# Attention of a graph layer taken two steps at a time, with three of four copies on ScalarE

## The chip, the cores and the metric

The kernel runs on one core of a Trainium2 chip. The core has five engines with a queue each: TensorE (PE; its weight loads are shown as PEld), VectorE (DVE), ScalarE (ACT), GpSimd (POOL), and SyncE (SP), which only issues transfers here. PE writes its results into PSUM, which has eight banks; DVE and ACT carry them from there to SBUF. The metric is the device time of one execution in microseconds (us), as the median over several runs. Times of single instructions come from one profiled execution.

## What is computed

There are 384 nodes with 1024 features. Two graph layers follow each other, each on a normalised and rectified input and with a residual. The first is an attention with 16 heads of 64 features and a mask made from the edges; the second is a relational convolution, two sublayers deep. Cut to what matters here:

```
h  = relu(layernorm(x))
q2 = (h wq' + bq) wiq' + biq ;  k2, v2 in the same way       (384 x 1024 each)
mask[src, dst] = softplus(w)[edge_type - 1], else -inf       (384 x 384)
attn = softmax(q2 k2' / 8 + mask)                            (per head, 384 x 384)
x  = x + (attn v2) wo' + bo
x  = x + relational_convolution(relu(layernorm(x)))          (counts A per relation and edge)
```

All numbers are fp32.

## The kernel before

Nodes are split into three blocks of 128. Queues are written out by hand for PE, POOL, SP and DVE, and from the attention on for ACT too: each engine works through its instructions in the order of the program text. So the order of calls in the text is the order in each queue.

The projections make q2, k2 and v2. The function `second_v` multiplies one half (512 columns) of one node block of v2, and gives back the copy out of PSUM.

The attention is then a run of 24 steps. Step g stands for pair p = g // 3 of heads (two heads, 0 and 1, in the two halves of the 128 partitions) and block m = g % 3. For each step there are these pieces of work:

- `scores(g)`: PE multiplies q2's block by k2 for both heads. The two products go to banks 0 and 1 for an even g, to banks 2 and 3 for an odd one. The two heads run in the array side by side.
- `exponents(g)`: DVE adds the mask to the scores and finds the extreme of each row in one operation per head (s, L576); ACT takes the exponential of each head (L579), and sums the rows. The result lies in one of eight slots for probabilities, in the tiles prA and prB.
- `normalise(g)`: DVE takes the reciprocal of the two sums (L584), and scales each head (L586).
- `turn_probs(g)`: PE transposes, for each head, block m of the three steps of pair p (three transposes each), into one of the banks 4, 5 and 6 in turn (L597). A copy brings the tile into a quarter of At (L598): on DVE for head 0, on ACT for head 1. Six transposes and two copies a step.
- `gather(g)`: PE multiplies v2's block m by the turned probabilities of each head (L608), and sums the three blocks of a pair in bank 7. After the third, ACT empties the bank into attT (L611), and the next pair starts in the same bank.

The loop runs over g with a lead of 5: it turns step g, does the exponentials of step g+5, normalises step g+4, computes the scores of step g+6, and multiplies step g-1 by v2. Ahead of it, steps 0 to 5 get their scores, in twos, with one piece of v2 after each of the first two pairs. Just before the last product, seven of eight parts of two blocks of ps_y = attT wo' are done (`multiply_o`, L615), which need the earlier pairs only.

In step 17 of the loop transfers are issued. SP loads w_x (which takes the place of q2 and k2), then five tiles w_c for the convolution (which take the place of w_o), then two slices of A, the table of edge counts. POOL loads the other slices and adds the second table to all of them. A has six slices, one for a relation, and its tables are filled by POOL's scatters (L266), which run through the whole attention.

After the attention come the output product, the normalisation, and the convolution, whose first sublayer needs the products ps_g (L840, L846) from PE, and from DVE the mixes of A (L326), the differences of weights (L787, L789, L795), and the additions into H (L853, L861, L863). POOL normalises the slices of A (L342).

## Time and profile before

| | |
|---|---|
| median of three runs | 737.99 us (736.06 to 738.41) |
| profiled execution | 735.77 us |
| its span, first to last instruction | 734.0 us |
| PE busy | 713.5 us (97%) |
| DVE busy | 472.9 us (64%) |
| ACT busy | 147.2 us (20%) |
| POOL busy | 323.3 us (44%) |
| first scores to the end of the last product with v2 | 237.4 to 317.7 us |
| first transposes to the first ps_y | 255.96 to 310.70 us |
| loads of A issued on SP | 388.1 us |

Times in the trace count from the start of the span. The chain is the work that ended last, followed back from the last instruction by what released each step. An fp32 product shows as two matmul records. A wait is put down to the releaser that came last. Shares of busy time are means over stages that differ much, so a change in one stage is read from that stage.

### The profile page before, as it was taken

What the parts mean: (1) busy time and instruction counts of PE and PEld (TensorE: products, weight loads), DVE (VectorE), ACT (ScalarE), POOL (GpSimd) and SP (SyncE); (2) the same over time, 40 slices, a digit from 0 to 9 for tenths busy, and PEclk for the clock granted to TensorE, in tenths of its full rate; (3) what the DMA queues carried; (4) which work ended last, traced back from release to release, by engine and by line L of the source; (5) the groups of instructions that cost most, each with busy time, mean ns of one, the idle gap of its engine ahead of it and who ended that gap; (6) DMA issues with size and microseconds to landing.
All of it is one profiled execution on the core that took longest, in us unless ns stands there. A gap on an engine that the chain in (4) does not pass through costs nothing.

```text
span 734.0 us, 8299 instructions
## 1 busy us (share of the span) xinstructions
PE 713.5 (97%) x3024; PEld 496.8 (68%) x3024; DVE 472.9 (64%) x1228; ACT 147.2 (20%) x338; POOL 323.3 (44%) x242
## 2 busy tenths in 40 slices
PE   8999989999999999999999999899999999999995
PEld 8759989999964444445995555555555555579943
DVE  6895897877504499625424779990187676506756
ACT  3201111111111477510131131100013111001100
POOL 1456777788886788587784454310000000030000
PEclk9999999999999999999999999999999999999999
DMA  7797766743447322623527953321003123700001
GB/s 296 261 346 231 221 182 209 212 148 115 116 119 240 59 1 2 215 0 47 127 2 169 312 163 129 129 83 46 0 1 107 66 85 129 271 29 1 1 29 57
DMA packets 40533, 90.96 MB, mean 124 GB/s; under 512 B 19644, under 2 KB 27680, under 8 KB 36270
## 3 DMA queue, kind: packets, MB, share of 16 engines
q1 hardware_dynamic: 18478, 79.62, 30.9%
q0 software_dynamic: 21008, 8.42, 10.4%
q10 hardware_dynamic: 1008, 2.41, 0.9%
q8 instruction: 23, 0.38, 0.2%
q14 instruction: 16, 0.13, 0.1%
HBM read 79.27 MB, written 11.16 MB: 123 GB/s over the span
## 4 chain that ended last, share of the span: by engine, by line
PE 86%; DVE 11%; ACT 1%; issue 1%; DMA 1%; DVEq 0%; ACTq 0%
PE ps_g L846 13%; PE ps_g L840 10%; PE ps_c L897 6%; PE ps_c L880 6%; PE ps_q L395 6%; PE ps_v L524 6%; PE ps_k L377 6%; PE ps_c L947 6%; PE ps_v L377 5%; PE ps_y L615 5%; PE ps_f L1054 4%; DVE same L250 3%; PE ps_q L377 3%; PE ps_x L377 3%; PE ps_o L608 2%; PE ps_s L563 2%
## 5 line engine op out<-in xcount | busy, mean ns | idle before, releaser
L266 POOL DMA_INDIRECT atab<-count,at x99 | 160.0, 1616 | 50.6 <-DMA atab<-count,at 26.2
L261 POOL DMA_INDIRECT mtab<-m_val,at x99 | 104.1, 1052 | 57.0 <-issue 24.4
L1041 POOL TENSOR_TENSOR x_sb<-x_sb,room 128x1024 f32<-128x1024 f32 x3 | 7.0, 2347 | 158.1 <-DMA room<-in_rows 158.1
L326 DVE SCALAR_TENSOR_TENSOR At<-A,small_sb,At 128x1152 f32<-128x1152 f32 x40 | 62.9, 1635 | 0.0
L840 PE MATMUL ps_g<-T,S 128*128 128x384 f32 x144 | 49.1, 486 | 0.0
L846 PE MATMUL ps_g<-w_c,XT 128*128 128x384 f32 x144 | 48.0, 487 | 0.0
L846 PE MATMUL ps_g<-w_c,XN 128*128 128x384 f32 x144 | 47.6, 486 | 0.0
L897 PE MATMUL ps_c<-At,H 128*128 128x384 f32 x144 | 46.6, 486 | 0.0
L395 PE MATMUL ps_q<-hT,w_q 128*128 128x384 f32 (+1 forms) x160 | 41.8, 422 | 1.4 <-ACT hT L90 1.4
L524 PE MATMUL ps_v<-w_v,v 128*128 128x512 f32 x96 | 41.9, 594 | 0.0
L840 PEld LDWEIGHTS ps_g<-T,S 128*128 128x128 f32 x144 | 27.4, 190 | 19.1
L897 PEld LDWEIGHTS ps_c<-At,H 128*128 128x128 f32 x144 | 27.4, 190 | 19.1
L846 PEld LDWEIGHTS ps_g<-w_c,XN 128*128 128x128 f32 x144 | 27.4, 190 | 19.1
L846 PEld LDWEIGHTS ps_g<-w_c,XT 128*128 128x128 f32 x144 | 27.2, 190 | 19.2 <-DVE H L861 0.6
L395 PEld LDWEIGHTS ps_q<-hT,w_q 128*128 128x128 f32 x160 | 28.5, 190 | 14.1 <-ACT hT L90 1.7
L377 PE MATMUL ps_k<-T,S 128*128 128x192 f32 x192 | 35.8, 330 | 0.0
L615 PE MATMUL ps_y<-w_o,attT 128*128 128x512 f32 x80 | 35.0, 595 | 0.0
L576 DVE CUSTOM_DVE_ANT_0 s<-ps_s,mask 128x384 f32<-128x384 f32 x48 | 24.5, 548 | 15.4 <-PE ps_s L563 15.4
L342 POOL TENSOR_TENSOR A<-A,rn 128x1152 f32<-128x1152 f32 x6 | 19.4, 3236 | 31.7 <-DVE rn L341 31.7
L524 PEld LDWEIGHTS ps_v<-w_v,v 128*128 128x128 f32 x96 | 18.0, 190 | 22.6 <-issue 22.6
L377 PEld LDWEIGHTS ps_k<-T,S 128*128 128x128 f32 x192 | 32.7, 194 | 0.0
L1054 PE MATMUL ps_f<-w_out,XN 128*128 128x512 f32 (+1 forms) x84 | 31.1, 531 | 0.0
(250 smaller groups left out, 1316.6 us busy)
## 6 DMA issues: line engine op xcount, KB each, us to landing
w_c<-in_basis SPq DMA_DIRECT2D x24, 768.0 KB, 6.2
atab<-zero SPq DMA_DIRECT2D x12, 576.0 KB, 8.2
A<-atab POOLq DMA_DIRECT2D x10, 576.0 KB, 9.8
w_c<-in_root SPq DMA_DIRECT2D x6, 768.0 KB, 5.5
w_q<-in_wq SPq DMA_DIRECT2D x4, 1024.0 KB, 11.8
w_q<-in_wiq SPq DMA_DIRECT2D x4, 1024.0 KB, 10.1
w_k<-in_wk SPq DMA_DIRECT2D x4, 1024.0 KB, 7.0
w_k<-in_wik SPq DMA_DIRECT2D x4, 1024.0 KB, 6.2
```

The source lines that it names most:

```text
L261: nc.gpsimd.indirect_dma_start(mtab[c // PER][:, :], bass.IndirectOffsetOnAxis(at[:, 0, c:c + 1], 0), m_val[:, c:c + 1], None)
L266: nc.gpsimd.indirect_dma_start(atab[0 if i < 18 - DEALT else i % 2][:, :], bass.IndirectOffsetOnAxis(at[:, 1, c:c + 1], 0), count[:, 1, c: ...
L326: nc.vector.scalar_tensor_tensor(At[:, b], A[:, r], w, At[:, b], ALU.mult, ALU.add)
L377: nc.tensor.matmul(ps, a[:, k, :], b[:, k, :], start=start and k == 0, stop=(k == 3), skip_group_check=not start)
L395: nc.tensor.matmul(ps[o][:, c], wt_[:, k, o * P:(o + 1) * P], src[:, k, c], start=(k == 0 and c.start == 0), stop=(k == KD - 1 and c.stop ...
L524: nc.tensor.matmul(ps, v[:, k, t * P:(t + 1) * P], w[k // 4][:, k % 4, :], start=(k == 0), stop=(k == KD - 1))
L615: nc.tensor.matmul(ps, attT[:, k, t * P:(t + 1) * P], w_o[half][k // 4][:, k % 4, :], start=(k == 0), stop=(k == KD - 1))
L840: nc.tensor.matmul(ps, x[:, c], y(c), start=start and c == 0, stop=(c == 2), skip_group_check=not start)
L846: nc.tensor.matmul(ps, block(XT, n, i)[:, c], w[c][:, i, o * HC:(o + 1) * HC], start=(first and c == 0), stop=(c == 2 and (i == 1 or ps is ...
L880: nc.tensor.matmul(pr[o], w[k // 2][:, k % 2, o * P:(o + 1) * P], XT[:, k, :], start=(k == 0), stop=(k == KC - 1 and l == L - 1))
L897: nc.tensor.matmul(pr[o], H_[:, b, n, o * P:(o + 1) * P], At[:, b, n, :], start=False, stop=(b == B - 1 and n == NT - 1))
L1054: nc.tensor.matmul(p, XT[:, k, t * P:(t + 1) * P], w[k // 2][:, k % 2, c0:c1], start=(k == 0), stop=(k == KC - 1))
```

## The change

The loop takes two steps at once. For an even g it turns steps g and g+1, does the exponentials of g+6 and g+7, normalises these two, computes the scores of g+8 and g+9, and multiplies steps g-2 and g-1 by v2. On DVE and ACT the copies of step g+1 stand between the exponentials of f = g+6 and those of f+1. Of the four copies of a double step DVE keeps one (step g+1, head 0). The slots for probabilities become twelve, the last four of them in slices 0 to 2 of A. All three blocks of v2's second half go between the first scores, and steps 0 to 7 get their scores ahead of the loop. The loads of A are issued after the loop; w_x and w_c stay in it, behind the last scores.

```diff
             for half in range(2):
                 w = [wload(wiv[half, j], "w_v2") for j in range(2)]
-                for t in range(NT - 2 * half):
+                for t in range(NT - NT * half):
                     second_v(half, t, w)()
...
         def probs(g):
-            i = g % 8
-            return (prA if i < 4 else prB)[:, 2 * (i % 4):2 * (i % 4) + 2, :]
+            i = g % 12
+            tile_ = (prA, prB, A.rearrange("p r t n -> p (r t) n"))[i // 4]
+            return tile_[:, 2 * (i % 4):2 * (i % 4) + 2, :]
...
-                (nc.scalar.copy if j else nc.vector.tensor_copy)(turned(g)[:, j, :], ps[:, :N])
+                copy = nc.vector.tensor_copy if g % 2 and j == 0 else nc.scalar.copy
+                yield lambda j=j, ps=ps, copy=copy: copy(turned(g)[:, j, :], ps[:, :N])
...
-        LEAD = 5
-        for f in (0, 2):
+        LEAD = 6
+        for f in (0, 2, 4):
             scores(f)
             scores(f + 1)
-            put_v = second_v(1, f // 2 + 1, w)
+            put_v = second_v(1, f // 2, w)
             for i in (f, f + 1):
                 exponents(i)
                 if i:
                     normalise(i - 1)
             put_v()
-        scores(4)
-        scores(5)
-        exponents(4)
-        normalise(3)
-        for g in range(STEPS + 1):
+        scores(6)
+        scores(7)
+        normalise(5)
+        for g in range(0, STEPS + 2, 2):
             f = g + LEAD
             if g < STEPS:
-                turn_probs(g)
+                copies = []
+                for i in (g, g + 1):
+                    for copy in turn_probs(i):
+                        copy() if i == g else copies.append(copy)
             if f < STEPS:
                 exponents(f)
-            if f - 1 in total:
-                normalise(f - 1)
-            if f + 1 < STEPS:
-                scores(f + 1)
+                copies.pop(0)()
+                copies.pop(0)()
+                exponents(f + 1)
+                normalise(f)
+                normalise(f + 1)
+            elif g < STEPS:
+                for copy in copies:
+                    copy()
+            if f + 2 < STEPS:
+                scores(f + 2)
+                scores(f + 3)
             if g == STEPS:
                 ps_y = [next_bank("ps_y", range(7)) for _ in range(2)]
                 multiply_o(ps_y[0], 0, 0, range(KD - 1))
             if g > 0:
+                gather(g - 2)
                 gather(g - 1)
-            if f + 2 == STEPS:
+            if f + 4 == STEPS:
...
-                for r in range(2):
-                    nc.sync.dma_start(A[:, r], tabs[0][r])
-                for r in range(R):
-                    nc.gpsimd.dma_start(A[:, r], tabs[1][r], accum_op=ALU.add)
...
+        for r in range(2):
+            nc.sync.dma_start(A[:, r], tabs[0][r])
+        for r in range(R):
+            nc.gpsimd.dma_start(A[:, r], tabs[1][r], accum_op=ALU.add)
```

## The prediction

> **What bounds the kernel now.** I read the page's busy times and chain first. TensorE (PE) is busy 97% and carries 86% of the chain, so the question is what PE waits for in the attention. Next the stretch that the diff touches, cut into stages (columns: stretch; time; PE, weight load, DVE, ACT, POOL busy; clock; DMA; GB/s):

> ```profile
> 237.36:255.96 18.60, 18.60 (x57) 7.98 (x57) 7.48 (x28) 8.15 (x20) 14.44 (x10) 1.00 0.40 58
> 255.96:270.60 14.64, 14.47 (x82) 7.06 (x80) 14.43 (x51) 10.80 (x32) 11.95 (x8) 1.00 0.20 1
> 270.60:299.97 29.37, 29.37 (x171) 13.64 (x169) 28.73 (x100) 23.31 (x67) 24.54 (x16) 1.00 0.23 2
> 299.97:304.30 4.33, 3.27 (x23) 1.67 (x21) 4.12 (x14) 3.18 (x9) 1.55 (x1) 1.00 0.94 321
> 304.30:310.70 6.40, 6.40 (x42) 3.34 (x40) 2.23 (x4) 2.50 (x5) 2.00 (x2) 1.00 1.02 396
> ```

> The third stage is the steady state, twelve steps of 2.447 us: PE is full, DVE 98%, ACT 79%. The chain in order of time (start, time, what) shows how a step is made, and one place where two steps' scores stand together:

> ```profile
> 237.43 1.49 PE ps_s L563 x8
> ...
> 282.11 0.80 PE ps_o L608 x4
> 282.91 0.81 PE ps_pT L597 x6
> 283.71 0.85 PE ps_s L563 x4
> ```

> A step's score group costs 0.85, two groups together 1.49: each change of kind costs PE about 0.1. In the single starts, scores follow each other 0.42 after a change and 0.316 within a run, transposes 0.165 and then 0.109, and the product with v2 0.367 after a change. From the last issue of a kind to the next kind it is 0.20 (transposes), 0.41 (scores), 0.42 (products).

> Last, rows of the timeline with the waits that PE already has (in brackets: idle time before, and its releaser), and the durations of the copies (least, median, most):

> ```profile
> 303.50 0.87 PE L608 MATMUL ps_o<-At,v 128*64 128x384 f32 x4 [1.06 <-ACT attT L611]
> ...
> L598 DVE COPY At<-ps_pT x24: 536/550/558, 257.2 to 309.7; 128x384 f32<-128x384 f32 x24
> L598 ACT COPY At<-ps_pT x24: 452/479/481, 257.3 to 310.1; 128x384 f32<-128x384 f32 x24
> ...
> 476.18 2.31 PE L880 MATMUL ps_c<-XT,w_c 128*128 128x384 f32 x6 [2.19 <-DVE H L853]
> ```

> The first row is the danger: the first product of a pair waits until ACT has emptied bank 7 of the pair before (L611). From start to next start in the trace: DVE's s (L576) 0.475, reciprocal 0.19, each L586 0.335, copy 0.467; ACT's exponential 0.61, copy and attT 0.463 (attT is done after 0.56). A waiting engine starts 0.05-0.06 after its releaser ends; ACT's exponential starts 0.66 after its s.

> [...] at 302.8 attT stands behind two exponentials although its product was long done. [...] 479 against 550 ns for a copy. [...] All pairs' products go through bank 7 alone, before and after. [...] 7 of the 48 L586 rows take 0.66-0.75 instead of 0.41.

> **The change, part by part.** *Work that only moves.* One second half of v2 (16 matmul records, 6.87) goes from before the scores into the score run, and steps 0-5 are now done under v2 instead of 0-4. The first scores start 6.87 earlier (230.5), the mask is ready at 232.6, so DVE loses 1 us under a v2 product of 7: nothing. The first transposes start after four score groups (1.49 each) and three v2 products (7.07 each): 230.49 + 27.15 = 257.64, against 255.96 before.

> *PE without waits.* A double step has 12 transposes (0.165 + 10x0.109 + 0.20 = 1.46), 4 score slots (0.42 + 2x0.316 + 0.41 = 1.47) and 4 product slots (0.367 + 2x0.316 + 0.42 = 1.42; the 0.316 is taken from the scores, at worst 0.367): 4.35 instead of 2x2.447 = 4.89. Over nine double steps with scores and three without this would save about 5.7.

> *The new loop DVE-PE.* DVE's order in a double step is s(f) twice, copy (step g+1, head 0), s(f+1) twice, normalise f and f+1. The copy needs the third transposed tile, and s(f+1) stands behind the copy. With the first transpose at 0: the tile's last transpose issues at 0.165 + 7x0.109 = 0.93 and ends at 1.20; copy 1.26; s(f+1) 1.73 and 2.20, the second has read its bank at 2.75. PE's scores f+3 overwrite that bank (a step's two heads use banks 0-1 or 2-3 by g's parity): head 1 starts at 2.80, second pass 3.22, products 3.63, next transposes 5.05. PE alone would be there at 4.35. So a double step takes 5.05 instead of 4.89. Behind the waiting copy stand s(f+1) and both normalisations, and for s(f+1) wait the scores, behind which stand the products. Before, the scores of a step overwrote the bank that DVE had read a step earlier, so the copy ahead of s did not matter to them.

> *The new load on ACT.* Copies 0.60 and 1.07, exponentials f 1.53 and 2.14 (they now stand behind copies that wait for this double step's transposes), copy 2.74, exponentials f+1 3.21 and 3.81, done 4.51. DVE then normalises f+1: reciprocal 4.56, free at 5.44; s(f+2) to 6.39, where the next copy was due at 6.31: 0.08 late. Hence about 5.1. The fourth transposed tile needs the first of three banks back (copy ends 1.08): 0.09, inside the loop's slack.

> *Bank 7.* Products come in twos (g-2, g-1), so in one double step of three a pair's last and the next pair's first stand side by side (2|3, 8|9, 14|15, 20|21). The last pass of the first issues at 4.00, ends 4.49, attT 4.54-5.10, next product 5.15 instead of 4.32: 0.83 on PE, three times; behind attT stand ACT's next copies, whose transposes are not there yet, so nothing else is late. At 14|15 no scores stand between (f+2 = 24), and attT stands behind the exponentials of step 23: ACT free 4.42, product 5.03 instead of 2.25: 2.8. Before, such waits cost 1.06 and 0.1.

> *Start.* The first double step has no products: 3.63. The second finds s(8) only at 5.45 after the first transpose (ACT's queue, as above): s(9) head 1 at 7.34, read at 7.89, its scores issue 7.94, products 8.77, next transposes 10.2. Together 10.2.

> *Sum.* 10.2; six double steps at 5.1 and two waits of 0.83: 32.3; the one of 14|15: 1.55 + 3.48 + 0.79 = 5.8; two without scores 2.98 each; the last 2.98 + 0.83 = 3.8. In all 58.1, so the first ps_y starts at 257.64 + 58.1 = 315.7, against 310.70: +5.0. Behind it two products instead of one: +0.6. The stage gets 5.6 longer.

> *Buffers.* Twelve slots for probabilities instead of eight and a lead of six steps instead of five: step g's transposes need the normalised steps up to g+3, made a double step earlier; the slot's last reader is two double steps back. No wait; if there were one, it would add to the loop on DVE.

> *Loads of A.* Their issue moves from step 17 to after the loop, on SP and on POOL; and A now lends three of its six slices as a third buffer for probabilities until the last transposes. In the trace SP issues the load at 388.1, released by POOL's scatters, which end at 387 and don't depend on PE; a loop that ends at 317 is 70 us early. SP's order (w_x, five w_c, A) and POOL's are the same. Nothing; without this cover each us would count. w_x leaves when the last scores are done, 297.5 against 298.7.

> *What is given back.* At 476.18 PE waits 2.19 for DVE, full since 427 and slowed there by POOL's work on A. POOL's times come from 388, not from PE, so with PE 5 us later they overlap less. But DVE's L863 at 449.08 waits for PE's product of 448.4, so only about 0.5 passes; at most 2.2. I take 0.5.

> Net +5.1. The profiled execution took 735.77 (span 734.0 and 1.8 around it): 740.9. The median of the runs is 738.0, 2.2 above: **743.1**.

> **The rivals.** *A, as above*, slower by 3 to 8: 743. *B, PE keeps the bound* and gains the run lengths: -5.7, 732. For it: DVE loses half a copy per step. Against it: scores f+3 are due 2.20 after the first transpose, and DVE can't free the bank before 2.75. It decides if DVE's s(f+1) came before the copy, which its queue does not allow. *C, the later slack eats it*: the whole 2.19 at 476 comes back and the waits are 2 smaller: 740, within 0.3% (2.2 us, about what a measurement tells from no change). *D, DVE is worse than its rows*: product slots gain nothing in a run (0.1 per double step, 1.0) [...]: +8, 746.

> **How the numbers follow.** A 0.70, B 0.06, C 0.09, D 0.15. The time is A's. The range runs from C's 739.5 to D's 746.5 and leaves out B and the far ends. Faster 0.06 (B), same 0.08, slower 0.86; a little of C is slower than 0.3%.

> **What would show it.** Right: double steps about 5.1 apart from first transpose to first transpose; the second head's scores released by DVE's s about 0.5-0.6 after PE could start them; product rows released by attT, three of about 0.8 and one of 2-3; ACT over 80% in the loop; A's load still at 388. In runs, scores at 0.32. Wrong: double steps under 4.6, or scores released by nothing; the wait at 476 gone and more; A's load later than 388; a wait on mask or prB before 257.6.

## The result

The changed kernel takes 743.32 us (median of 8 runs, 739.81 to 744.0), the kernel before, run beside it, 738.2 us (8 runs, 735.95 to 739.19): a ratio of 1.0071 with an interval of 1.005 to 1.0091. It is 5.1 us slower, where 5.1 was forecast. The profiled execution took 742.36 us, with a span of 740.3, against 735.77 and 734.0. In the experiments some executions are slower (of e9's 20, six took 754.5 to 761.0 us and the others 743.1 to 754.2), and the ratios to the kernel before leave these out, while the medians are those of all executions.

A double step is two steps taken together, and 14|15 is the place where step 14 ends one pair of heads and step 15 begins the next. The attention of the changed kernel, cut like that of the kernel before: v2 and the first scores; the first two double steps; the six in the middle; the first part of the one at the change of pairs 14|15; the rest of the loop; the last two products of steps with v2, with the pieces of ps_y ahead of them (columns: stretch; time; PE, weight load, DVE, ACT, POOL busy with records; clock; DMA; GB/s):

```profile
230.00:257.16 27.16, 27.16 (x82) 11.63 (x81) 14.14 (x52) 11.36 (x29) 20.71 (x13) 1.00 0.44 91
257.16:267.31 10.15, 9.45 (x50) 5.10 (x49) 8.63 (x31) 7.37 (x22) 8.18 (x6) 1.00 0.20 1
267.31:299.45 32.14, 30.78 (x170) 15.71 (x168) 25.75 (x90) 23.97 (x70) 26.96 (x18) 1.00 0.25 5
299.45:304.41 4.96, 2.69 (x19) 1.48 (x17) 4.17 (x16) 4.10 (x12) 1.18 (x1) 1.00 0.94 352
304.41:316.81 12.40, 11.72 (x65) 6.54 (x65) 2.13 (x5) 5.22 (x11) 6.51 (x5) 0.86 0.53 168
316.81:324.45 7.64, 7.64 (x24) 3.06 (x22) 0.00 (x0) 0.00 (x0) 6.42 (x5) 1.00 0.25 0
```

Before, twelve steps took 29.37 with PE full, DVE at 98% and ACT at 79%. Now twelve steps take 32.14 with PE at 96%, DVE at 80% and ACT at 75%. No engine is full any more, so what sets the length has to be looked for in the waits of one engine for another. The fifth row holds something else: a mean clock of 0.86.

The chain in order of time (start, time, what) shows that the longer runs are there:

```profile
282.09 1.44 PE ps_o L610 x8
283.53 1.65 PE ps_pT L598 x12
285.18 1.99 PE ps_s L564 x8
287.17 0.82 PE ps_o L610 x4
```

Two steps' products take 1.44 where one took 0.80, and the transposes of two steps 1.65. The scores of two steps take 1.99, but they stood at 1.49 where two groups followed each other without a wait: half a microsecond is lost inside this run. The timeline of DVE at that place shows to what:

```profile
284.06 0.55 DVE L577 CUSTOM_DVE_ANT_0 s<-ps_s,mask 128x384 f32<-128x384 f32 x1
...
284.70 0.56 DVE L600 COPY At<-ps_pT 128x384 f32<-128x384 f32 x1
285.18 0.55 DVE L577 CUSTOM_DVE_ANT_0 s<-ps_s,mask 128x384 f32<-128x384 f32 x1
...
285.65 0.55 DVE L577 CUSTOM_DVE_ANT_0 s<-ps_s,mask 128x384 f32<-128x384 f32 x1
```

The copy stands between s(f) and s(f+1), and waits for its transposes, of which the first issues at 283.46. The second s(f+1) therefore ends at 286.20. By the single starts in the trace, head 0 of the scores f+3 issues at 285.86. Head 1, which takes the bank that s has just read, would follow 0.01 behind without a wait, as it does in the passes of the step f+2 ahead of it (285.112 and 285.119, 285.539 and 285.546), and comes at 286.26. That is 0.39 late; the two heads are then out of step, and their second passes cost another 0.1. The list of waits (engine, tile, line, releaser: us in all, times, longest) shows this loop and the one of bank 7:

```profile
PEld ps_s L564 <- DVE top L577: 5.9, 18, 0.9
...
PE ps_o L610 <- ACT attT L613: 4.3, 4, 2.3
```

PE's timeline has the places (idle time and releaser in brackets):

```profile
263.13 2.81 PE L564 MATMUL ps_s<-k,q 64*128 64x384 f32 x8 [0.67 <-DVE top L577]
...
272.50 0.87 PE L610 MATMUL ps_o<-At,v 128*64 128x384 f32 x4 [0.68 <-ACT attT L613]
...
283.46 1.72 PE L598 MATMUL ps_pT<-ident,A 128*128 128x128 f32 x12
...
288.65 0.87 PE L610 MATMUL ps_o<-At,v 128*64 128x384 f32 x4 [0.68 <-ACT attT L613]
...
304.41 1.28 PE L610 MATMUL ps_o<-At,v 128*64 128x384 f32 x4 [2.27 <-ACT attT L613]
...
316.01 0.87 PE L610 MATMUL ps_o<-At,v 128*64 128x384 f32 x4 [0.68 <-ACT attT L613]
```

Four waits for attT, three of 0.68 and one of 2.27 at the change of pairs 14|15. ACT's timeline shows what attT stood behind there:

```profile
302.57 0.63 ACT L580 ACTIVATE A<-s,top 128x384 f32<-128x384 f32 x1
...
303.18 0.61 ACT L580 ACTIVATE A<-s,top 128x384 f32<-128x384 f32 x1
...
303.78 0.57 ACT L613 ACTIVATE attT<-ps_o,cols_sb 128x384 f32<-128x384 f32 x1
```

The product was issued by 301.65; its copy out starts 2.1 later, after the exponentials of step 23. In the kernel before it stood behind these too, and PE waited 1.06 for it; now the wait is twice as long. But the row at 304.41 takes 1.28 instead of 0.87, which nothing above explains. The windows of one microsecond behind it do (eighth column from the stretch on: the clock):

```profile
304.00:305.00 1.00, 0.59 (x4) 0.20 (x4) 0.83 (x3) 0.35 (x1) 0.00 (x0) 0.86 1.03 393
305.00:306.00 1.00, 1.00 (x6) 0.39 (x3) 0.00 (x0) 0.00 (x0) 0.00 (x0) 0.50 1.07 430
...
308.00:309.00 1.00, 1.00 (x9) 0.40 (x9) 0.39 (x1) 0.48 (x1) 0.00 (x0) 0.93 1.06 404
```

The copies (least, median, most in ns; first to last) last as long as before, 480 and 558 against 479 and 550, now 36 to 12:

```profile
L600 ACT COPY At<-ps_pT x36: 456/480/487, 257.7 to 314.6; 128x384 f32<-128x384 f32 x36
...
L600 DVE COPY At<-ps_pT x12: 546/558/559, 258.4 to 314.1; 128x384 f32<-128x384 f32 x12
```

Behind the attention everything comes 6.75 later (the first ps_x at 361.54 against 354.79), up to the wait for H in the convolution:

```profile
482.45 1.99 PE L893 MATMUL ps_c<-XT,w_c 128*128 128x384 f32 x5 [2.00 <-DVE H L866]
```

It came at 476.18 after a wait of 2.19 before, so 6.27 are left, and the end is 6.27 later too. SP's load of A has not moved with PE at all, though its issue stands behind the loop now: 386.85 against 388.1.

```profile
386.85 0.91 SPq L669 DMA_DIRECT2D A<-atab  x2
```

### The profile page after: what moved, and what is told of

Its sections match the earlier page's. It is cut to its first block, busy times and chain, and to the rows that moved or that the text cites. A ratio compares the mean times of both kernels' runs of the same rounds, so it can differ in the third digit from the quotient of the medians.

```text
span 740.3 us, 8312 instructions
## 1 busy us (share of the span) xinstructions
PE 715.5 (97%) x3024; PEld 499.6 (67%) x3024; DVE 466.5 (63%) x1216; ACT 150.7 (20%) x350; POOL 321.2 (43%) x242
## 4 chain that ended last, share of the span: by engine, by line
PE 86%; DVE 10%; ACT 2%; issue 1%; DMA 0%; DVEq 0%; ACTq 0%
PE ps_g L859 13%; PE ps_g L853 10%; PE ps_c L910 6%; PE ps_c L893 6%; PE ps_v L524 6%; PE ps_q L395 6%; PE ps_k L377 6%; PE ps_c L960 6%; PE ps_v L377 5%; PE ps_y L617 5%; PE ps_f L1067 4%; DVE same L250 3%; PE ps_q L377 3%; PE ps_s L564 3%; PE ps_x L377 3%; PE ps_o L610 2%
## 5 line engine op out<-in xcount | busy, mean ns | idle before, releaser
L326 DVE SCALAR_TENSOR_TENSOR At<-A,small_sb,At 128x1152 f32<-128x1152 f32 x40 | 62.9, 1636 | 0.0
L853 PE MATMUL ps_g<-T,S 128*128 128x384 f32 x144 | 49.1, 486 | 0.0
L524 PE MATMUL ps_v<-w_v,v 128*128 128x512 f32 x96 | 42.2, 595 | 0.0
L853 PEld LDWEIGHTS ps_g<-T,S 128*128 128x128 f32 x144 | 27.4, 190 | 19.1
L342 POOL TENSOR_TENSOR A<-A,rn 128x1152 f32<-128x1152 f32 x6 | 19.0, 3160 | 36.1 <-DVE rn L341 36.1
L524 PEld LDWEIGHTS ps_v<-w_v,v 128*128 128x128 f32 x96 | 18.0, 190 | 22.7 <-issue 22.7
```

Source lines behind the costliest of these rows:

```text
L326: nc.vector.scalar_tensor_tensor(At[:, b], A[:, r], w, At[:, b], ALU.mult, ALU.add)
L524: nc.tensor.matmul(ps, v[:, k, t * P:(t + 1) * P], w[k // 4][:, k % 4, :], start=(k == 0), stop=(k == KD - 1))
L853: nc.tensor.matmul(ps, x[:, c], y(c), start=start and c == 0, stop=(c == 2), skip_group_check=not start)
```

## Experiments

The intervals of the ratios of all versions in pairs of steps overlap, so their totals don't tell them apart. Total times on the chips of the experiments scatter by 10 us and more, and most of it comes from ahead of the attention: the first product of v2 (L524) starts between 207.9 and 227.5 in the twelve profiles. In the kernel before, PE's waits in the product ps_k come to 4.3 us in its first profile and to 12.8 on the third chip, where the mean clock is 0.987 against 0.996. So I read a **stage**, from that product (some expectations call it the first of v2's second half) to where ps_y resumes behind the last products with v2: 107.90 before, 115.15 after. Within it I read the **loop**, first transpose to first ps_y (54.74 and 59.65), and the times from first transpose to first transpose of two steps. All of them, worked out from the starts in the traces:

```
                      twelve double steps, the last up to ps_y                       loop   stage
before                4.47 5.04 5.14 4.89 4.89 4.89 4.89 4.89 4.89 4.33 3.20 3.20   54.74  107.90
after                 3.64 6.51 5.99 5.08 5.08 5.99 5.08 5.08 6.00 4.11 3.09 3.99   59.65  115.15
e1 single steps       4.10 4.89 4.89 4.89 4.89 4.89 4.89 4.89 4.05 3.20 3.20 3.20   52.00  106.20
e2 copy behind s      3.09 6.35 5.58 4.58 4.94 5.58 4.58 5.00 5.58 3.09 3.09 3.99   55.48  110.97
e3 no bank wait       3.64 6.42 5.37 5.08 5.08 5.37 5.08 5.08 3.38 3.73 3.09 3.38   54.73  110.22
e4 wait filled        3.64 6.29 5.99 5.08 5.09 5.99 5.08 5.08 5.58 3.09 3.09 3.99   58.00  113.49
e5 old copies         4.41 6.62 6.75 5.85 5.85 6.75 5.85 5.85 5.90 4.53 3.12 4.02   65.49  120.99
e6 e2 and e3          3.08 6.35 4.87 4.62 4.90 5.12 4.58 4.91 3.38 3.73 3.09 3.38   52.02  107.52
e7 after, again       3.64 6.50 5.98 5.09 5.08 5.98 5.09 5.08 6.26 3.74 3.09 3.99   59.53  115.03
e8 single, again      4.10 4.89 4.89 4.89 4.89 4.89 4.89 4.89 4.05 3.20 3.20 3.20   52.00  106.20
e9 before, again      4.56 4.89 4.97 4.89 4.89 4.89 4.89 4.89 4.89 4.33 3.20 3.20   54.51  107.68
e10 single, third     4.10 4.89 4.89 4.89 4.89 4.89 4.90 4.89 4.05 3.20 3.20 3.20   52.01  106.21
```

**Single steps, all else as changed.** Twelve slots, the lead of 6, the place of v2 and of A's loads stay; steps are taken one at a time with the old split of the copies.

```diff
-                copy = nc.vector.tensor_copy if g % 2 and j == 0 else nc.scalar.copy
+                copy = nc.scalar.copy if j else nc.vector.tensor_copy
...
-        scores(7)
         normalise(5)
-        for g in range(0, STEPS + 2, 2):
+        for g in range(STEPS + 1):
             f = g + LEAD
             if g < STEPS:
-                copies = []
-                for i in (g, g + 1):
-                    for copy in turn_probs(i):
-                        copy() if i == g else copies.append(copy)
+                for copy in turn_probs(g):
+                    copy()
             if f < STEPS:
                 exponents(f)
...
+            if f - 1 in total:
+                normalise(f - 1)
+            if f + 1 < STEPS:
+                scores(f + 1)
...
             if g > 0:
-                gather(g - 2)
                 gather(g - 1)
-            if f + 4 == STEPS:
+            if f + 2 == STEPS:
```

> The changed kernel with its lead of six steps, its twelve slots, its three v2 blocks among the first scores and its late loads of A, but one step at a time and with the copies split as before (head 0 on DVE, head 1 on ACT). Theory (the taking of two steps together costs the time, the rest of the change does not): steps stay at 2.45 us, one step fewer has scores and exponentials in the loop, and the wait behind the last exponentials is shorter, so 1.5 us below before: 736.5. Rival (the longer lead, the third buffer in A or the late loads cost it): 742 to 744, as the changed kernel.

741.82 us against 742.88 of the kernel before on this chip (0.998, 0.9956 to 1.0003), so the gain of 1.5 that was expected is not shown in the total. The stage takes 106.20, 1.70 less than before. So none of the parts of the change that this version keeps costs anything in the attention: the loss is in taking two steps at once. The new split of the copies, which it does not keep, is tried further down. The gain has two places: the wait of 1.06 for attT is gone, and the first three double steps take 4.10, 4.89, 4.89 instead of 4.47, 5.04, 5.14.

**DVE's copy behind s(f+1).** Only this order changes. It makes the same copies on the same engines.

```diff
                 exponents(f)
-                copies.pop(0)()
-                copies.pop(0)()
+                copies.pop(1)()
                 exponents(f + 1)
+                copies.pop(0)()
                 normalise(f)
```

> The changed kernel with DVE's one copy of a double step moved behind the s of step f+1. Theory (loop copy, s, scores on PE sets 5.1 us, with ACT's queue close behind it): double steps fall to about 4.87, the mean of a 4.5 and a 5.3, and the stage gets 1.7 us shorter than in the changed kernel: 741.6. Rival (only ACT's queue sets the double step): it stays at 5.1, 743.3. Rival (PE alone sets it): falls to 4.4, 738.

747.48 us, ratio 1.0061 (1.0021 to 1.0101). The double steps without a change of pair, called plain here, fall from 5.08 to 4.58 and about 5.0 in turn, 4.78 in the mean, where 4.87 was expected. The loop falls to 55.48, against 58.00 in the changed kernel at full clock (e4 in the table). The wait of the scores for DVE is more than halved in the list of waits, against 5.9 us, 18 times, in the changed kernel:

```profile
PEld ps_s L564 <- DVE top L577: 2.5, 11, 0.8
```

The copy ahead of s(f+1) is shown as a cause, by reordering it alone.

**No wait at bank 7.** The copies into attT for pairs 0, 2, 4 and 6 read v2 instead of the bank, so that the next pair need not wait for them; what these pairs' products sum up to is not used.

```diff
-                nc.scalar.activation(attT[:, p, :], pso.pop(p)[:, :N], AF.Identity, bias=cols_sb[:, BIV + p:BIV + p + 1])
+                o = pso.pop(p)[:, :N] if p % 2 else v2[:, 0, :N]
+                nc.scalar.activation(attT[:, p, :], o, AF.Identity, bias=cols_sb[:, BIV + p:BIV + p + 1])
```

> The changed kernel, but for the pairs 0, 2, 4 and 6 attT is filled from v2 in place of bank 7, by an operation of the same length on ACT; the products of those pairs are made, and left unused. So the four waits of a first product behind attT are gone, and all else stays. Theory: 3 x 0.83 us less, and at steps 14 and 15 of the 2.3 to 2.8 about 1.5 less, since the next step then waits for ACT in its place: 4.1 less. If the clock that was halved for 3.4 us behind the long wait also stays up, 1.6 less on top. Together 737.6 to 739.2. Rival (the waits only take up time that the loop would lose anyway): under 1 us less, 742.5.

746.68 us, ratio 1.0042 (1.0021 to 1.0064). The stage falls to 110.22, which is 3.3 below the changed kernel's at full clock (113.49, the next experiment). It is less than the 4.1 expected. The double steps with a change of pair take 5.37, not 5.08: each keeps 0.29. The list of waits says for what:

```profile
PEld ps_o L610 <- PE ps_o L610: 2.9, 4, 0.7
```

The first product of a pair waits for PE's own last product into that bank, with no reader between. It is a wait of the program: in the trace its weight load waits for a semaphore that this last product raises at its end. Whether the chip needs it was not tried. And at 14|15 the next double step gives back 0.64 (3.73 instead of 3.09), as its transposes wait 0.61 for a copy on ACT.

**The wait at 14|15 filled.** Three products that nobody reads stand between the two steps' products there, so PE is not idle.

```diff
                 gather(g - 2)
+                if g == 16:
+                    for j in range(2):
+                        fill_bank = bank(j, "ps_fill")
+                        for _ in range(2 - j):
+                            nc.tensor.matmul(fill_bank[:, :N], ones, mask8[:, 0, :], start=True, stop=True)
                 gather(g - 1)
```

> The changed kernel with three more products of PE (384 columns each, into banks 0 and 1, read by nobody) in the wait between steps 14 and 15. They take about 2 us of a wait of 2.3 to 2.8 and delay nothing. Theory (that wait halves PE's clock for 3.4 us behind it): the clock stays up there, and executions that lost 1.6 us don't: median 741.7 to 742.3, mean granted clock from 0.992 to 0.994. Rival (the halving has nothing to do with the wait): no change, 743.3.

749.1 us, ratio 1.0078 (1.0049 to 1.0107). PE's timeline:

```profile
310.25 2.20 PE L663 MATMUL ps_fill<-mask,ones 128*128 128x384 f32 x6
312.58 0.87 PE L610 MATMUL ps_o<-At,v 128*64 128x384 f32 x4
```

The product behind takes 0.87 again, the clock stays at 1.00, and the two double steps take 5.58 + 3.09 where the changed kernel took 6.00 + 4.11: the halved clock cost 1.44. By itself this run did not settle the cause, because e2, whose wait of 2.27 was not filled, kept its clock too. That is taken up below.

**Half of the copies on DVE again**, in pairs of steps.

```diff
-                copy = nc.vector.tensor_copy if g % 2 and j == 0 else nc.scalar.copy
+                copy = nc.scalar.copy if j else nc.vector.tensor_copy
```

> The changed kernel, in double steps, but with the copies split as before: head 0 of both steps on DVE, head 1 on ACT. Theory (DVE's copies stand ahead of s, and s ahead of PE's scores): now the copy of step g, too, holds s(f) until this double step's first tile is turned, so s(f+1) comes 0.7 later; double steps 5.84, with a wait at bank 7 6.7; from the first v2 product to the resumption of ps_y 119 us, where the changed kernel had 115.2 and the one before 107.9. Rival (ACT's queue sets the double step): with one copy less on ACT it falls to 4.7.

762.98 us in a single execution. Plain double steps take 5.85, those with a change of pair 6.75, and the stage 120.99, a stretch of halved clock behind a wait of 2.56 among it (the transposes from 325.23 on last 0.42 instead of 0.27, and the loop's mean clock is 0.97). The scores wait longer for DVE:

```profile
PEld ps_s L564 <- DVE top L577: 8.7, 28, 0.6
```

So fewer copies on DVE help a paired loop, and a loop set by ACT alone, in which this would have been a gain, is refuted.

**Both causes removed** (e2 and e3 together; the same products are not used).

> Both edits in one: DVE's copy behind s(f+1), and attT of the pairs 0, 2, 4 and 6 filled from v2 in place of bank 7 (their products are left unused). Theory (the loop through DVE and the waits at bank 7 are separate terms, and ACT's queue is what is left): double steps 4.6 and 5.0 in turn, none with a wait over 0.4; from the first v2 product to the resumption of ps_y 107.5 to 109, no better than the 107.9 of the kernel before. Rival (the two hide each other): under 1 us less than with either edit alone, 109.5 to 111. Rival (PE alone is left): double steps 4.4, 104.

754.5 us in a single execution. The stage over its whole length:

```profile
227.45:334.97 107.52, 105.75 (x449) 50.96 (x447) 59.11 (x191) 53.07 (x147) 73.53 (x47) 1.00 0.40 87
```

Against 113.49 it has lost 5.97; e2 alone lost 2.52 and e3 alone 3.27, together 5.79. The two causes are separate and add up. With both gone, pairs of steps are only level with the kernel before (107.90), and behind single steps (106.20). Its transposes wait 4.4 for ACT's copies, in 13 places, so I take the rest to be ACT's queue; no run isolates it.

**The changed kernel and single steps, once more on another chip.**

> The changed kernel once more, beside the next one on the same chip. Theory: as on record, 5 us above the kernel before, ratio 1.007; from the first v2 product to the resumption of ps_y 113.5 us where the clock stays up behind the wait of steps 14 and 15, 115.2 where it is halved there.

> The single steps with the longer lead once more. Theory: 1.5 us below the kernel before, ratio 0.998, and 6.5 to 7 us below the changed kernel; from the first v2 product to the resumption of ps_y 106.2 us, as in the first look. Rival (the first look was chance): no different from the kernel before.

The changed kernel took 758.68 us (ratio 1.0088, 1.0017 to 1.0158) and single steps 751.68 (1.007, 1.0024 to 1.0115). The stages are 115.03 and 106.20, as on the first chips. But the total of single steps is now above the kernel before, against the 0.998 expected.

**The kernel before and single steps on a third chip.**

> The kernel before, unchanged, profiled on a third chip. If the stretch from the first product of v2's second half to the second half of ps_y belongs to the order of the work, it is again 107.9 us within 0.3, whatever the total; if chips differ in it, it moves with the total by several us, and the readings of single and paired steps from this stretch would be of no use.

> Single steps with everything else of the change, beside the kernel before on the same chip. The same stretch is again 106.2, 1.7 below the kernel before. If the parts ahead of the attention take what they take before, the total is 1.2 to 1.7 lower, a ratio of 0.998; the rival is that 16 more products ahead of the scores or the later arrival of weights costs that back ahead of the attention: then the ratio is at or above 1 and the first of those products starts later than in the kernel before on this chip.

The kernel before came to 752.43 us (1.002, 0.9986 to 1.0054, against its own runs there) and single steps to 754.26 (1.0042, 1.0002 to 1.0082). The stage as one window, for the kernel before:

```profile
225.21:332.89 107.68, 106.61 (x449) 48.28 (x447) 65.04 (x204) 49.98 (x135) 73.02 (x48) 1.00 0.41 92
```

And for single steps:

```profile
218.00:324.21 106.21, 106.21 (x448) 47.90 (x447) 65.80 (x204) 50.82 (x135) 75.11 (x50) 1.00 0.44 100
```

The stage keeps its length on the chips measured: 107.90 and 107.68 before, then 106.20, 106.20 and 106.21 in single steps, in which PE is never idle. So single steps win 1.5 to 1.7 us there, and three comparisons of the whole (0.998, 1.007, 1.0042) don't show it. The rival named for this is not supported either: in the one profile of each on the third chip the first product of v2 started earlier with single steps (218.00) than before (225.21). One place where the gain can go is seen in the first single-step profile, in its waits behind the attention:

```profile
PE ps_g L848 <- DVE H L863: 4.7, 1, 4.7
PE ps_cnt L338 <- POOL sum L333: 1.2, 1, 1.2
```

There PE came early and waited for DVE's H and POOL's sum. On the third chip the first of these waits was 0.7, and on the second chip it was absent, so it is no rule. Whether single steps shorten the whole stays open; no version here is shown to beat the kernel before.

**The clock behind a wait.** In the changed kernel the clock is 0.50 from 304.72 to 308.13, behind the wait of 2.27 at 14|15. Two more profiles have a wait of 2.27 at the same place. In e7 it lies from 316.48 to 318.75, and the clock is 0.50 from 318.60 on:

```profile
314.50:318.60 4.10, 1.98 (x14) 0.93 (x11) 3.34 (x14) 4.00 (x12) 0.50 (x1) 1.00 0.98 384
318.60:322.01 3.41, 3.26 (x13) 2.08 (x14) 0.61 (x2) 0.72 (x3) 1.25 (x1) 0.50 1.05 409
```

In e2 it lies from 303.77 to 306.04, and the clock stays at 1.00:

```profile
302.50:305.02 2.52, 1.27 (x7) 0.43 (x7) 2.30 (x8) 2.52 (x9) 0.10 (x1) 1.00 1.01 424
305.02:308.43 3.41, 2.39 (x16) 1.48 (x16) 1.27 (x4) 1.83 (x5) 0.00 (x0) 1.00 1.04 404
308.43:311.80 3.37, 3.37 (x24) 1.96 (x24) 0.76 (x2) 1.92 (x5) 1.57 (x1) 1.00 0.99 322
```

The wait for H has both outcomes too. In the first profile of the kernel before it was 2.19, with the clock at 1.00 behind it (478.23 to 481.64), and in the changed kernel 2.00, with 1.00 from 475 to 500. For the kernel before on the third chip it was 2.00, up to 490.93, and a clock of 0.51 followed:

```profile
487.88:491.29 3.41, 1.41 (x5) 0.59 (x4) 3.41 (x4) 0.00 (x0) 1.31 (x1) 1.00 0.76 306
491.29:494.70 3.41, 3.41 (x7) 1.83 (x6) 3.38 (x4) 0.00 (x0) 0.00 (x0) 0.51 0.01 4
```

So waits of one length went both ways: half a clock followed 2.27 twice out of three times, and 2.00 in one of these two profiles. I take the wait at 14|15 for the cause of the halving in the changed kernel, because the loop's clock is 1.00 where that wait was filled (e4) or gone (e3 and e6). That is a reading of these runs: e2 kept its clock with the wait in place, and no run shows what sets it apart. Nor does every execution seem to have the halving. The shortest of the changed kernel, 739.81, had a mean clock of 0.999, which leaves no room for 3.41 us at half clock; the other seven had 0.991 to 0.994.

## Why the prediction was right

**Work that only moves.** The first transposes were due at 257.64 and came at 257.16, with v2 starting 0.49 earlier than before (209.31 against 209.80), for reasons upstream. From v2's start it is 47.85, forecast 47.84. Single steps with the same moves shorten the stage, so nothing of it costs there.

**The loop DVE-PE.** Plain double steps at 5.1: measured 5.08. The trace has its links too. From the first transpose at 283.46 the copy starts after 1.24 (forecast 1.26), the second s(f+1) ends after 2.74 (2.75), head 1 issues after 2.80 (2.80) and the products after 3.64 (3.63). PE could have issued head 1 only 0.39 earlier, not 0.5 to 0.6, because the transposes take 1.65 and not 1.46. The claim that the copy ahead of s(f+1) makes the time, and not PE, ACT or the number of copies, was tested three ways: moved behind, 4.78; more copies on DVE, 5.85; both causes removed, 4.58 to 4.9. The bare PE time of 4.35 was never reached; that ACT's copies come next, as the step on ACT's load had it, fits the waits in e6 but is not isolated. One sign did not come: ACT was to be over 80% busy in the loop, and is at 75%, below the 79% of before.

**Bank 7.** 0.83 for each ordinary change of pair: measured 0.91 (5.99 - 5.08). The place 14|15: forecast 5.8, measured 5.58 in e4 at full clock. One part of the step was incomplete: it put the whole wait on attT, but 0.29 of each remains when nobody reads the bank, for PE's own last product. At 14|15 the second product was to issue 5.03 after the first transpose, and came after 4.79 (304.41 against 299.62).

**Start and sum.** The first two double steps 10.2, measured 10.15; the two without scores 2.98 each, measured 3.09; the last 3.8, measured 3.99. The loop was to take 58.1: measured 59.65, of which 1.44 is the halved clock, so 58.2 without it. Behind it +0.6: measured 0.64 (6.75 - 6.11).

**Buffers and A's loads.** No row of waits in the loop names a slot's reader or the mask, and the load of A is at 386.85. **Given back:** 0.5, measured 0.48 (6.75 - 6.27), though the wait itself fell only from 2.19 to 2.00. As forecast, DVE waits for PE's product at its third addition into H (L876 at 455.33, after 1.31 idle, against L863 at 449.08), and so most of the delay passes. How much DVE is slowed by POOL's work on A can be read from the mixes (L326) in the trace of before: they take 1.32 to 3.78 where an operation of POOL (L332, L333, L342) overlaps them, and 1.40 to 1.41 where none does.

**The profiled execution** was to take 740.9 and took 742.36. The 1.46 are: halved clock +1.44, earlier start upstream -0.49, rest of the loop +0.11, what lies around the span 2.09 instead of 1.77, +0.32, and +0.08 of small terms. So the sum was right by its mechanism, while one profiled execution differs by a term that the prediction did not have. The median, 743.32 against 743.1, can't be divided so, because it is not recorded where the clock was halved in the executions without a profile. That it came within 0.2 is partly luck: the prediction had no term for the halved clock, which cost 1.44 in this profile.

**The rivals.** B (PE keeps the bound): refuted, PE waits, and even with both causes removed the stage is level with before. C (the later slack eats it): 0.48 of 2.19, refuted. D (product slots that gain nothing in a run, and six long rows of L586 that each cost the loop 0.3): refuted in both halves, in-run products follow at 0.322 to 0.323 against 0.373 for the first one after a change, and the six double steps are at 5.08 and 5.99, within 0.01 of each other. The prediction counts seven long rows of L586; the trace of before has six of 0.66 and more, and the changed kernel four of 0.64 to 0.74 (L587), so that double steps of equal length hold rows of both kinds; why a row is long is not shown.

## What to carry to other kernels

Longer runs of one kind save PE only its changes of kind, here at most 0.54 of 4.89 us by the single starts, and cost distance: ask for each buffer that the second of two steps reuses who must have emptied it, and what stands ahead of that reader in its queue. In a kernel whose engines are nearly full, price a regrouping by following one double step through every queue; sums of busy time would have called this a gain. And look at the clock behind single long waits of PE: the wait of 2.27 was paid twice here, once as a wait and once as the 1.44 lost at half clock behind it.

## What was not expected of the hardware

Behind a wait of 2.27 us PE's clock was 0.50 for 3.41 us in the changed kernel, which cost 1.44 us there, and 0.50 for 3.41 us again in e7. In e2 it was 1.00 behind a wait of the same length. Behind a wait of 2.00 us it was 0.51 over 3.41 us in e9, and 1.00 in the changed kernel.

The length of the attention's stage repeats within 0.22 us on chips whose total times differ by 10 to 15 us.
